# A graph network's attention layer: neighbour sums of all heads moved across the first head's steps

## The chip, the cores and the metric

One core of one Trainium2 chip. The metric is the device time of one execution of the whole kernel in microseconds (us): 1761.85 us, the median of three runs (1759.87 to 1763.0).

## The reference, cut to what matters

Four layers over a graph of 2708 nodes with 512 features: a normalisation with ReLU, then a graph layer whose result is added to `x`. Layers 0, 1 and 3 multiply the adjacency with features. Layer 2 is attention with 8 heads of 64 features:

```python
Wh = jnp.einsum('nd,hdo->hno', x, W)
f1 = jnp.einsum('hno,ho->hn', Wh, a1)
f2 = jnp.einsum('hno,ho->hn', Wh, a2)
e = jax.nn.leaky_relu(f1[:, :, None] + f2[:, None, :], negative_slope=0.2)
e = jnp.where(adj[None, :, :] > 0, e, -9e15)
attention = jax.nn.softmax(e, axis=-1)
h_prime = jnp.einsum('hnm,hmo->hno', attention, Wh)
```

The exponential of a leaky sum splits into products of exponentials of `f1` and of `f2`, joined by a maximum. So the kernel needs no exponential per pair of nodes: it makes a tile of weights by a maximum and a multiplication with the adjacency, and takes the softmax's denominator as a sum over the same tiles.

## The kernel before, in words

All four layers run on the one core, and the adjacency is kept on the chip as bytes (`vT`, turned, six groups). Nodes are cut into `NC = 22` chunks of 128, the last of 20.

**The dense stage of attention** (`stages2`, from `aggregate` and `staged`) goes over the chunks. `product2` multiplies by `W`, ScalarE evicts the product (`wh`, L1085), VectorE and POOL each multiply it with one of the vectors `a1`, `a2` (L1090), POOL folds its half (L1096), and `sums2` reduces (L1107) and clamps (L1109) into `f12`. `rows2` then takes exponentials for the first `EARLY = 11` chunks, turns them into a row on TensorE (`row2`, L1120: transpose into PSUM, copy L1122 on ScalarE, transfer L1123 to `rT` in memory), and loads that row spread over all partitions as `rb` (L957). At `LATE = 17` and after, it starts the first head: `scale` and `make` of its first steps run while the dense stage ends.

**The heads** are walked in `steps`: pairs of a unit `u` (a head, or one half of the columns of the first and of the last head) and a chunk `m`. The first head has two units of 22 steps, s0 to s21 with 1408 columns and s22 to s43 with 1300. Unit 2 is the first with the full width of 2708 columns. For each step:

- `scale` (L1028, L1030; ScalarE) scales the chunk's features and a constant block by `ef`: tile `whs`, four buffers;
- `make` (L1043; VectorE) writes the weights `t2 = max(rb, ec) * vT`: `TILES = 4` buffers;
- `compare` (L1061; ScalarE) makes a mask of comparisons, in middle heads only, for the chunks in `BY_SIDE`, 17 of the 22;
- `multiply` (L1243; TensorE) adds the products to `av` and `sums` in PSUM;
- `multiply_sides`, in the middle heads, gets the rest of the sums from the masks of the step before.

**The neighbour sums** serve the middle heads. Each chunk in `BY_SIDE` needs its `vT` in 16-bit form: four casts for four column ranges (`mask`, L1330, tiles of tag `x` with `XBUFS = 5` buffers), then eight matmuls (`count_neighbors`, L1342) against `parts2`, into two PSUM banks `adj_sums` that stay open from the first chunk to the last. `split` (L1292 to L1313) prepares `parts2`: it cuts `ef` and `ec*ef` each into three 16-bit parts (`parts`), with casts on ScalarE and subtractions on VectorE, then rearranges them.

**The tails**: the last chunk, of 20 rows, of the six middle heads is handled as one tile of 120 rows. `load_tails` loads it by many small transfers on SP's queue, `exp_tails` (L987 to L989) takes exponentials and scales, `make_tails` (L992) makes its weights. Step s44 is the first to use them.

**What sets the order.** The Python loop over steps issues `scale(s+3)`, `make(s+3)`, `compare(s+1)`, `multiply(s)`, and then what the table `plan` has under `s` (`behind(s, fn, ...)`). A scheduler then orders each engine's instructions by their issue order and readiness; each engine runs its list in that order. `tc.issue_after(ins)` keeps the instructions in its block behind `ins` on the same engine. PSUM has eight banks (pool `ps`): a half unit holds three, a full unit five, the neighbour sums two, and each row transpose one.

Of the kernel before, what the change touches and what calls it, by code (L numbers as in the profile page):

```python
# [8 lines left out]
F32 = mybir.dt.float32  # L9
F32R = mybir.dt.float32r  # L10
BF16 = mybir.dt.bfloat16
# [3 lines left out]
AF = mybir.ActivationFunctionType  # L15
ALU = mybir.AluOpType
# [4 lines left out]
P = 128  # L21

R = 128
# [21 lines left out]
def fast_layers(  # L45
# [36 lines left out]
    nc = tc.nc  # L82
    N, D = x_in.shape
    H, _, O = w2.shape
    NC = -(-N // R)
# [26 lines left out]
    EARLY = NC // 2  # L112
# [10 lines left out]
    common = ctx.enter_context(tc.tile_pool(name="common", bufs=2))  # L123
# [279 lines left out]
    vT = []  # L403
# [69 lines left out]
    with ExitStack() as ring_ctx:  # L473
# [31 lines left out]
        with tc.tile_pool(name="l0", bufs=2) as wk, ExitStack() as ctx_l0:  # L505
            units = [(g, m) for g in range(len(groups)) for m in range(NC)]
            tiles, acc, sums, xs = {}, {}, {}, {}
# [210 lines left out]
            first = [first_dense(lag, fn) for lag, fn in dense(x_in, product0, rows_of=paired)]  # L718
# [182 lines left out]
    BY_SIDE = [m for m in range(NC - 1) if m % 5 != 2]  # L901


    STEEP = 2.0**62
    ABOVE = 1.0 + 2.0**-21
# [32 lines left out]
    ef = at.tile([R, NC, H], F32, name="ef")  # L938
    ec = at.tile([R, NC, H], F32, name="ec")
    eb = at.tile([R, NC, H], F32, name="eb")  # L940
    parts = at.tile([R, NC * H * 8 + S], BF16, name="parts")
    nc.gpsimd.memset(parts, 0.0)
    parts_of = parts[:, : NC * H * 8].rearrange("p (m h k) -> p m h k", h=H, k=8)

    parts2 = at.tile([R, len(BY_SIDE), 2, H, 3], BF16, name="parts2")
    nc.gpsimd.memset(parts2, 0.0)
    one6 = at.tile([R, S], F32, name="one6")
    nc.gpsimd.memset(one6, 0.0)
    nc.gpsimd.memset(one6[:, 6:7], 1.0)
    row, weight, wh, whs, acc, sides, made = {}, {}, {}, {}, {}, {}, []  # L950

    def load_row1(h, lo, hi):

# [65 lines left out]
    def scale(s):  # L1019

        u, m = steps[s]
        h, q = units[u][0], rows(m)
        if in_tails(u, m):
            whs[s] = tails_w[:LINES, middle.index(h)]
            return
        t = at.tile([R, O + S], F32, name="whs", bufs=4)
        by = ef[:q, m, h : h + 1]
        nc.scalar.activation(t[:q, :O], wh.pop((u, m))[:q], AF.Copy, scale=by)  # L1028
        if not by_side(u, m):
            nc.scalar.activation(t[:q, O:], one6[:q], AF.Copy, scale=by)  # L1030
        whs[s] = t[:q]

    def make(s):
        u, m = steps[s]
        h, lo, hi = units[u]
        q = rows(m)
        g, k = where[m]
        if in_tails(u, m):
            weight[s] = tails_row[:LINES]
            made.append(made[-1])  # L1040
            return
        t = at.tile([R, N], F32, name="t2", bufs=TILES)
        ins = nc.vector.scalar_tensor_tensor(  # L1043
            t[:q, : hi - lo],
            row[h][:q, lo:hi],
            ec[:q, m, h : h + 1],
            vT[g][:q, k, lo:hi],
            op0=ALU.max,
            op1=ALU.mult,
        )  # L1050
        weight[s] = t[:q]
        made.append(ins.ins)
# [77 lines left out]
        nc.scalar.activation(ec[:, cs], f12[:R, cs, H:], AF.Exp, scale=SLOPE2 - 1.0)  # L1130


    LATE = NC - 5
    early_rows = [(0, EARLY // 2 + 1), (EARLY // 2 + 1, EARLY)]

    def rows2(c):
        for first, end in early_rows:
            if c == end - 1:
                exps_nodes(slice(first, end))
            for n in range(2):  # L1140
                if first <= first + 2 * (c - end + 1) + n < end and c >= end - 1:
                    row2(first + 2 * (c - end + 1) + n)
        if c == EARLY + 1:
            load_row1(*units[0])

        if c == LATE:
            exps2(slice(0, EARLY))
            load_wh(0)
            load_wh(GROUP)
        if LATE < c <= LATE + 3:  # L1150
            scale(len(made))
            make(len(made))

    def save_last2(c):
        if c < len(spans[-1]):
# [131 lines left out]
                    t[j * step : j * step + height, : b - a],  # L1287
                )

    def split():  # L1290

        nc.scalar.mul(eb, ec, -STEEP * ABOVE)  # L1292
        rest = common.tile([P, D], F32, name="rest", tag="t", bufs=3)
        rest = rest[:R, : NC * H].rearrange("p (m h) -> p m h", h=H)
        for i in range(2):
            e = ef
            if i:
                nc.vector.tensor_tensor(rest, ec, ef, ALU.mult)
                e = rest
            for k in range(3):  # L1300
                part = parts_of[:, :, :, 3 * i + k]
                nc.scalar.copy(part, e)
                if k < 2:
                    nc.vector.tensor_tensor(rest, e, part, ALU.subtract)
                    e = rest
        for i, heads in enumerate((slice(1, H), slice(1, H - 1))):
            kinds = sorted({m % 5 for m in BY_SIDE})
            for r in kinds:
                ms = [m for m in BY_SIDE if m % 5 == r]
                src = parts_of[:, r : ms[-1] + 1 : 5, heads, 3:6]  # L1310
                at_i = [BY_SIDE.index(m) for m in ms]
                assert at_i == list(range(at_i[0], at_i[-1] + 1, len(kinds)))
                nc.scalar.copy(  # L1313
                    parts2[:, at_i[0] : at_i[-1] + 1 : len(kinds), i, heads], src
                )


    fourths = [0, cut // 2, cut, (cut + N) // 2, N]
    counted, masks = [], {}

# [3 lines left out]
    def mask(i, j):  # L1324
        m = BY_SIDE[i]
        q = rows(m)
        g, k = where[m]
        own = slice(fourths[j], fourths[j + 1])
        t = masks[i, j] = common.tile([P, D], F32, name="x", bufs=XBUFS).bitcast(BF16)
        nc.scalar.copy(t[:q, : own.stop - own.start], vT[g][:q, k, own])  # L1330

    def count_neighbors(i):
        m = BY_SIDE[i]
# [37 lines left out]
    def behind(s, fn, *args):  # L1371
        plan.setdefault(s, []).append((fn, args))
# [3 lines left out]
    for c in range(EARLY, NC):  # L1376
        behind(4 + (c - EARLY) // 2, row2, c)
    behind(10, load_row1, *units[1])
    behind(9, split)
    behind(12, load_tails)  # L1380
    behind(18, exp_tails)
    behind(22, make_tails)
    behind(30, load_l3_weights)
    behind(30, spread_nodes)
    for u in range(2, len(units)):
# [3 lines left out]
        behind((u + 1) * NC - 1, evict, u, 0)  # L1389
        behind(min((u + 1) * NC, len(steps) - 1), evict, u, 1)  # L1390
    for i in range(len(BY_SIDE)):
        first = 11 + 7 * i // 4
        for j in range(4):
            behind(first + j // 2, mask, i, j)
        behind(first + 2, count_neighbors, i)
# [17 lines left out]
    for s in range(len(steps)):  # L1413
        if s == (len(units) - 3) * NC + 1:
            tails_ctx.close()
            e3_ctx = ctx.enter_context(ExitStack())
            e3 = e3_ctx.enter_context(
                tc.tile_pool(name="e3", bufs=2, side="right", reuse_waits="tile")
            )
        if s + 6 < len(steps) and (s + 6) % NC % GROUP == 0:  # L1420
            load_wh(s + 6)
        if s + 3 < len(steps):
            scale(s + 3)
            make(s + 3)
        if s + 1 < len(steps):
            compare(s + 1)
        multiply(s)
        multiply_sides(s - 1)
        for fn, args in plan.pop(s, ()):
            if fn in (load_l3_weights, spread_nodes, split):  # L1430
                with tc.issue_after(made[s]):
                    fn(*args)
            else:
                fn(*args)
# [742 lines left out]
```

## Time and profile before

| | |
|---|---|
| time, median of three | 1761.85 us |
| profiled execution | 1762.76 us, its span 1761.0 us |
| mean granted TensorE clock | 0.994 |
| TensorE busy | 1729.5 us (98%) |
| VectorE busy | 1307.4 us (74%) |
| ScalarE busy | 849.1 us (48%) |
| POOL busy | 249.2 us (14%) |
| makes, L1043 | 214, together 510.7 us |
| casts for the neighbour sums, L1330 | 68, from 801.7 to 912.2 us |
| neighbour-sum matmuls, L1342 | 136, from 849.7 to 913.6 us |
| first matmul of s0 | 819.57 us |

In a view in order of time, a line has the start in us, the time from its start to its end, the engine, the source line, the operation, the tile written and those read, partitions and elements, and how many instructions were merged; in brackets stands how long the engine had been idle before and what ended that. In a list of waits, a line has the waiting engine and line, what it waited for, and the total in us, the times, and the longest. In a list of groups, the figures after the bar are busy time in us, mean ns of one, and the idle time before with what ended it. A busy TensorE isn't TensorE at its peak.

### The profile page before, as it was taken

To read this page: it belongs to the slowest core of one execution; us is meant where nothing else is said; L and a number is where in the kernel's file an instruction comes from. 1 tells how busy PE (TensorE), PEld (TensorE's weight loads), DVE (VectorE), ACT (ScalarE), POOL (GpSimd) and SP (SyncE) were. 2 spreads that over 40 slices of the span, in tenths; PEclk is the share of its full clock that TensorE was granted. 3 is DMA by queue.
4 is the path that set the end of the run, shared out by engine and by line. 5 is a ranking of instruction groups with operands and counts; after the bars stand their busy time and mean duration, and the time that the engine had idled before them with its cause. 6 is when DMAs were issued, how large, how long until landed. Compare 5 with 4: busy or idle time off the path is not lost.

```text
span 1761.0 us, 29469 instructions
## 1 busy us (share of the span) xinstructions
PE 1729.5 (98%) x11280; PEld 1055.1 (60%) x11280; DVE 1307.4 (74%) x1889; ACT 849.1 (48%) x1547; POOL 249.2 (14%) x252
## 2 busy tenths in 40 slices
PE   8999999999999999999999999999999999999998
PEld 5567777744458887644474554434434455588886
DVE  8649888955555556888799999999999777633334
ACT  5447666722210000265888888888794566400000
POOL 1003323311111112255000000000001222100000
PEclk9999999999999999999999999999999999999999
DMA  8436666455551111333420220122022444313221
GB/s 295 140 95 207 205 197 185 145 113 122 121 141 49 48 49 54 110 128 102 127 61 16 62 63 22 50 64 59 16 65 69 136 136 133 112 32 109 76 72 41
DMA packets 167227, 177.37 MB, mean 101 GB/s; under 512 B 84127, under 2 KB 106591, under 8 KB 166060
## 3 DMA queue, kind: packets, MB, share of 16 engines
q1 hardware_dynamic: 144428, 131.99, 26.5%
q10 hardware_dynamic: 18808, 33.37, 5.1%
q0 software_dynamic: 3840, 10.03, 1.4%
q8 instruction: 90, 1.47, 0.3%
q14 instruction: 61, 0.50, 0.1%
HBM read 111.64 MB, written 55.36 MB: 95 GB/s over the span
## 4 chain that ended last, share of the span: by engine, by line
PE 84%; DVE 10%; DMA 2%; ACT 2%; issue 1%; POOL 0%; SPq 0%; ACTq 0%; DVEq 0%; POOLq 0%
PE acc L424 32%; PE av L1243 19%; PE nb_ps L187 8%; PE sums L1243 5%; DVE t L1043 4%; PE h_ps L187 4%; PE self_ps L187 4%; PE line_ps L187 4%; PE wh_ps L187 3%; PE hT_ps L245 2%; DVE cum L555 2%; PE fused_ps L370 1%; DMA x<-x 1%; PE av_ps L1196 1%; PE adj_sums L1342 1%
## 5 line engine op out<-in xcount | busy, mean ns | idle before, releaser
L1043 DVE SCALAR_TENSOR_TENSOR t<-rb,ec,vT 128x2708 f32<-128x2708 f32 (+2 forms) x214 | 510.7, 2449 | 17.3 <-PE sums L1243 15.3
L1243 PE MATMUL av<-t,whs 128*32 128x451 f32 (+5 forms) x4432 | 430.2, 513 | 4.6 <-DVE f L1109 1.4
L424 PE MATMUL acc<-halves,kt 128*128 128x512 f32 x1848 | 426.3, 390 | 3.5 <-DVE kt L847 3.2
L424 PEld LDWEIGHTS acc<-halves,kt 128*128 128x128 f32 x1848 | 345.1, 188 | 81.4 <-DVE kt L847 8.6
L1061 ACT ACTIVATE b<-t,eb 128x2708 bf16<-128x2708 f32 (+1 forms) x119 | 285.1, 2396 | 36.6 <-DVE t L1043 36.5
L1243 PEld LDWEIGHTS av<-t,whs 128*32 128x32 f32 (+1 forms) x4432 | 171.1, 110 | 178.4 <-issue 140.4
L424 PE MATMUL acc<-halves,ar 128*128 128x512 f32 x924 | 246.2, 417 | 2.4 <-ACT ar L549 2.2
L424 PEld LDWEIGHTS acc<-halves,ar 128*128 128x128 f32 x924 | 173.3, 189 | 62.4 <-issue 22.2
L223 ACT ACTIVATE ln_rs<-ln_mv,eps 128x1 f32<-128x1 f32 x88 | 25.5, 294 | 319.2 <-DVE ln_mv L221 310.7
L847 DVE SCALAR_TENSOR_TENSOR kt<-lastr,index,vT 128x512 fp32r<-128x512 int16 (+3 forms) x154 | 112.4, 742 | 75.8 <-PE acc L424 75.4
L1494 DVE CAST kt<-vT 128x512 fp32r<-128x512 uint8 (+3 forms) x154 | 56.4, 368 | 131.4 <-PE acc L424 131.2
L1210 POOL TENSOR_SCALAR z<-y 128x512 f32<-128x512 f32 x22 | 44.1, 2003 | 644.6 <-DMA aT<-avT 520.3
L555 DVE TENSOR_TENSOR_SCAN cum<-ai,deg 128x512 int16<-128x512 int32 (+2 forms) x110 | 130.7, 1196 | 0.0
L598 ACT ACTIVATE cum<-cum,limit 128x512 int16<-128x512 int16 (+3 forms) x132 | 88.1, 668 | 50.1 <-DVE deg L563 48.0
L219 DVE BATCH_NORM_STATS2 ln_st<-x 128x6 f32<-128x512 f32 x88 | 60.3, 687 | 51.6 <-DMA x<-x 38.4
L1028 ACT ACTIVATE whs<-wh,ef 128x64 f32<-128x64 f32 x214 | 72.8, 344 | 52.6 <-PE sums L1243 18.7
L1243 PE MATMUL sums<-t,whs 128*32 128x325 f32 (+4 forms) x952 | 92.2, 448 | 0.0
L187 PE MATMUL nb_ps<-wfn,hT 128*128 128x512 f32 x168 | 78.1, 609 | 2.1 <-ACT hT L247 2.1
L187 PE MATMUL wh_ps<-w2s,hT 128*128 128x512 f32 x168 | 75.9, 594 | 0.2 <-ACT hT L247 0.2
L187 PE MATMUL h_ps<-w0s,hT 128*128 128x512 f32 x168 | 75.8, 594 | 0.0
L187 PE MATMUL nb_ps<-wn,hT 128*128 128x512 f32 x168 | 75.6, 592 | 0.0
L187 PE MATMUL self_ps<-wfs,hT 128*128 128x512 f32 x168 | 75.6, 592 | 0.0
(210 smaller groups left out, 1907.8 us busy)
## 6 DMA issues: line engine op xcount, KB each, us to landing
x<-x SPq DMA_DIRECT2D x105, 256.0 KB
ai<-in_adj SPq DMA_DIRECT2D x84, 256.0 KB
x<-x ACTq DMA_DIRECT2D x84, 256.0 KB
x<-in_x SPq DMA_DIRECT2D x42, 256.0 KB
rb<-rT SPq DMA_DIRECT2D x7, 1354.0 KB
wh<-whd SPq DMA_DIRECT2D x63, 96.0 KB
packed<-two POOLq DMA_DIRECT2D x44, 128.0 KB, 3.1
whd<-wh SPq DMA_DIRECT2D x21, 256.0 KB
```

Of the source, the lines that this page charges most:

```text
L187: nc.tensor.matmul(po[:n], lhsT[:, f, :n], w[:, f, :], start=(f == 0), stop=(f == NF - 1))
L219: nc.vector.bn_stats(st[:n], xc[:n])
L424: nc.tensor.matmul(acc[:R], weight[:, k * R : (k + 1) * R], parts[:, i, :], start=(m == 0 and i == 0), stop=(m == NC - 1),)
L555: nc.vector.tensor_tensor_scan(cum[:n, :gw], ai[:n, :gw], ai[:n, :gw], 0.0 if g == 0 else deg[:n, m : m + 1], op0=ALU.add, op1=ALU.max,)
L598: nc.scalar.activation(cum[:n, :gw], cum[:n, :gw], AF.Sign, bias=limit[:n], scale=-1.0, accum_out=signs[:n, m, g : g + 1],)
L847: nc.vector.scalar_tensor_tensor(by_chunk(kt, cs), lastr[:, cs[0] * R : (cs[-1] + 1) * R].rearrange("p (c r) -> p c r", r=R), index[:R, m ...
L1028: nc.scalar.activation(t[:q, :O], wh.pop((u, m))[:q], AF.Copy, scale=by)
L1043: ins = nc.vector.scalar_tensor_tensor(t[:q, : hi - lo], row[h][:q, lo:hi], ec[:q, m, h : h + 1], vT[g][:q, k, lo:hi], op0=ALU.max, op1=AL ...
L1061: nc.scalar.activation(b[:q, : hi - lo], weight[s][:, : hi - lo], AF.Sigmoid, bias=eb[:q, m, h : h + 1], scale=STEEP,)
L1210: nc.gpsimd.tensor_scalar(z, y, 0.0, None, op0=ALU.min)
L1243: nc.tensor.matmul(p[j * S : (j + 1) * S, : b - a], lhsT, rhs[:, part * size + a : part * size + b], start=(s % NC == 0), stop=(s % NC == ...
L1494: nc.vector.tensor_copy(by_chunk(kt, cs), pattern(m, cs))
```

## The change

- `split` takes a range of chunks and runs twice: for the first 11 from `rows2`, in the dense stage at chunk `LATE + 1 = 18`, and for the other 11 at its former place, step 9.
- The neighbour sums of chunk `i` of the 17 begin at step `1 + 39 i // 16` in place of `11 + 7 i // 4`: two casts in that step, two in the next, the matmuls in the step after. They then stretch from s1 to s42 where they stretched from s11 to s41.
- The fourth of each chunk's casts (650 columns) goes to VectorE, into a tile of its own (`mask`, two buffers).
- Casts are kept behind the scaling and the make of the step two later (`scaled`, `made`).
- `exp_tails` is due at step 30 in place of 18, `make_tails` at 36 in place of 22.

```diff
     def scale(s):
...
-        nc.scalar.activation(t[:q, :O], wh.pop((u, m))[:q], AF.Copy, scale=by)
+        ins = nc.scalar.activation(t[:q, :O], wh.pop((u, m))[:q], AF.Copy, scale=by)
         if not by_side(u, m):
-            nc.scalar.activation(t[:q, O:], one6[:q], AF.Copy, scale=by)
+            ins = nc.scalar.activation(t[:q, O:], one6[:q], AF.Copy, scale=by)
+        scaled[s] = ins.ins
...
+    def split(first, end):
+
+        cs = slice(first, end)
+        nc.scalar.mul(eb[:, cs], ec[:, cs], -STEEP * ABOVE)
+        rest = common.tile([P, D], F32, name="rest", tag="t", bufs=3)
+        rest = rest[:R, : (end - first) * H].rearrange("p (m h) -> p m h", h=H)
+        for i in range(2):
+            e = ef[:, cs]
+            if i:
+                nc.vector.tensor_tensor(rest, ec[:, cs], e, ALU.mult)
+                e = rest
+            for k in range(3):
+                part = parts_of[:, cs, :, 3 * i + k]
+                nc.scalar.copy(part, e)
+                if k < 2:
+                    nc.vector.tensor_tensor(rest, e, part, ALU.subtract)
+                    e = rest
+        for i, heads in enumerate((slice(1, H), slice(1, H - 1))):
+            kinds = sorted({m % 5 for m in BY_SIDE})
+            for r in kinds:
+                ms = [m for m in BY_SIDE if m % 5 == r and first <= m < end]
+                src = parts_of[:, ms[0] : ms[-1] + 1 : 5, heads, 3:6]
+                at_i = [BY_SIDE.index(m) for m in ms]
+                assert at_i == list(range(at_i[0], at_i[-1] + 1, len(kinds)))
+                nc.scalar.copy(
+                    parts2[:, at_i[0] : at_i[-1] + 1 : len(kinds), i, heads], src
+                )
...
         if LATE < c <= LATE + 3:
             scale(len(made))
             make(len(made))
+        if c == LATE + 1:
+            split(0, EARLY)
...
-    def split():
...
     def mask(i, j):
...
+        n = own.stop - own.start
+        if j == 3:
+            t = masks[i, j] = tails.tile([P, fourths[1]], BF16, name="mask", bufs=2)
+            nc.vector.tensor_copy(t[:q, :n], vT[g][:q, k, own])
+            return
         t = masks[i, j] = common.tile([P, D], F32, name="x", bufs=XBUFS).bitcast(BF16)
-        nc.scalar.copy(t[:q, : own.stop - own.start], vT[g][:q, k, own])
+        nc.scalar.copy(t[:q, :n], vT[g][:q, k, own])
...
-    behind(9, split)
+    behind(9, split, EARLY, NC)
     behind(12, load_tails)
-    behind(18, exp_tails)
-    behind(22, make_tails)
+    behind(30, exp_tails)
+    behind(36, make_tails)
...
     for i in range(len(BY_SIDE)):
-        first = 11 + 7 * i // 4
+        first = 1 + 39 * i // 16
         for j in range(4):
             behind(first + j // 2, mask, i, j)
         behind(first + 2, count_neighbors, i)
...
             if fn in (load_l3_weights, spread_nodes, split):
                 with tc.issue_after(made[s]):
                     fn(*args)
+            elif fn is mask:
+                with tc.issue_after(scaled[s + 2]), tc.issue_after(made[s + 2]):
+                    fn(*args)
             else:
                 fn(*args)
```

More of the change, by code (lines that the diff above doesn't have):

```diff
@@ L949, in fast_layers @@
     nc.gpsimd.memset(one6[:, 6:7], 1.0)
-    row, weight, wh, whs, acc, sides, made = {}, {}, {}, {}, {}, {}, []
+    row, weight, wh, whs, acc, sides, made, scaled = {}, {}, {}, {}, {}, {}, [], {}
     def load_row1(h, lo, hi):
@@ L1288, in evict @@
                 )
-    def split():
[L1292 to L1315, printed above, removed]
     fourths = [0, cut // 2, cut, (cut + N) // 2, N]
```

## The prediction

> **What bounds the kernel now.** I read the page first (section 5: which engines carry attention), then the busy times by stage, then order of time around the first head. Steps are numbered s0 to s43 (two units of 22, half a head each), "make" is the VectorE weight tile of a step (L1043), "count" the eight neighbour-sum matmuls of one chunk (L1342), "cast" the byte-to-bf16 copy that feeds it (L1330).
>
> VectorE in order of time; the middle stretch and the start of the steady one:
>
> ```profile
> 879.55 9.79 DVE L1043 SCALAR_TENSOR_TENSOR t<-rb,ec,vT 128x1300 f32<-128x1300 f32 x6 [6.19 <-PE sums L1243]
> ...
> 912.05 29.59 DVE L1043 SCALAR_TENSOR_TENSOR t<-rb,ec,vT 128x2708 f32<-128x2708 f32 x10 [0.36 <-PE sums L1243]
> ```
>
> From 912.05 us, the make of s45 (first full-width tile), VectorE does not stop: the busy view gives it 387.95 of the 388 us from 912 to 1300, and it goes on to 1345. So the middle heads are VectorE's, and what the first head costs is the time at which VectorE can start s45. Before that it is held by TensorE, which has to give back one of the four weight tiles. Why TensorE is late (waits from 815 to 940, then TensorE and ScalarE in order of time):
>
> ```profile
> DVE t L1043 <- PE sums L1243: 15.3, 14, 6.2
> PE adj_sums L1342 <- ACT x L1330: 3.5, 7, 1.1
> ```
>
> ```profile
> 852.24 0.31 PE L1342 MATMUL adj_sums<-x,parts 128*24 128x352 bf16 x1
> 853.67 0.31 PE L1342 MATMUL adj_sums<-x,parts 128*24 128x352 bf16 x1 [1.11 <-ACT x L1330]
> ...
> 868.70 0.73 PE L1342 MATMUL adj_sums<-x,parts 128*24 128x352 bf16 x8
> ...
> 872.04 5.81 PE L1342 MATMUL adj_sums<-x,parts 128*24 128x325 bf16 x18 [0.24 <-ACT x L1330]
> 877.53 1.41 PE L1243 MATMUL av<-t,whs 128*32 128x325 f32 x16
> ```
>
> ```profile
> 871.24 5.99 ACT L1330 CAST x<-vT 128x650 bf16<-128x650 uint8 x9
> ```
>
> The 18 matmuls "busy" for 5.81 us run beside nine casts back to back for 5.99 us: they are paced by the casts. Elsewhere eight of them cost 0.28 to 0.30 us. TensorE loses about 8 us here, ScalarE being full and behind.
>
> [...]for 704 and 650 elements, the rows say 771 and 730, spaced 0.67. [...]
>
> ```profile
> L1494 DVE CAST kt<-vT 128x512 fp32r<-128x512 uint8 x88 | 37.3, 425 | 98.3 <-PE acc L424 98.3
> L1494 DVE CAST kt<-vT 128x128 fp32r<-128x128 uint8 x22 | 4.8, 226 | 4.8 <-PE acc L424 4.8
> ```
>
> 199 ns for 384 elements is 0.52 ns each[...]. The 16-element clamp L1109 takes 0.20 us alone and 1.23 behind a make while POOL works (812.19)[...].
>
> **Ledger of before.** From TensorE's start of s4 (828.70) to the end of s43 (917.28) is 88.6 us. Work: 18 steps of unit 0 at 1.775 (856.87 to 860.70 holds two and a count of 0.28) = 31.95; 22 of unit 1 at 1.64 = 36.1; 17 counts at 0.29 = 4.9; eleven row transposes at 0.22 (2.22 us for a step with two) = 2.45. Sum 75.4, so 13.2 us are stalls: 1.1 before the first count (849.1 to 850.5), 2.6 around the second (852.2 to 855.1), 7.9 between s21 and s22 (868.6 to 877.5 less 3.75 counts), 0.9 at 902, rest small. Every one waits for casts or for parts on ScalarE.
>
> **The change, part by part**, by the built order of each engine's instructions.
>
> *Casts spread and a fourth moved.* ScalarE loses 17 casts x 0.67 = 11.4 us. From 852 on it has 30 scalings x 0.45, 24 casts x 0.67, 1.1 for tails, 1.2 for evictions: 32 to 40 us of 53, so its cover for the rest is 13 us. VectorE gains 17 casts of 650 elements: 226 + 522 x 0.52 = 498 ns, less 0.08 overlap (makes of 1.67 follow each other by 1.596) = 0.42. Its bounds: [...]0.76 at one (159 + 650 x 1.05, the makes' slope, - 80); I take 0.42, as the nearest row has byte input too. With them VectorE needs 1.596 + 0.17 per step in unit 0 against TensorE's 1.775 + 0.12, and 1.49 + 0.17 in unit 1 against 1.64 + 0.12: still below, by 0.1, so hidden behind TensorE, but barely. If that cover goes, each cast costs its 0.42.
>
> *First half of the parts in the dense stage.* Five operations of 88 columns on VectorE, between 806 and 826: rows of 343 and 488 at 176 columns less 88 x 1.04, about 0.31 each, 1.55 in all. In this stretch VectorE is the chain (it waits for nothing but 0.80), so they count in full. ScalarE gets two short ones ahead of the row copy that precedes the first transfer of rb, against one scaling pair moved back: nothing to 0.2. The waits matter more. ScalarE's cast of the fourth rest now stands in front of the eviction wh L1085 of chunk 20, and it needs VectorE's subtraction behind two reductions, about 822.9; in before that eviction came at 818.40. Queued behind it are the evictions and the POOL product of chunk 20 (821.48 before, about 823.95 now), then POOL's remaining 1.1 + 1.26 + 0.72, on which VectorE's last reduction and the make of s4 wait: 826.89 becomes about 829.35.
>
> *First count at s3.* On TensorE it stands between s3 and s4, and its fourth operand is a VectorE cast placed behind the make of s5: 829.35 + 1.6 + 0.1 + 1.6 + 0.42 = 833.0. So s4 starts at 833.3 where it started at 828.70: **4.6 us paid**. Everything on TensorE queues behind that count. If its operand came in time I would pay 2 less.
>
> *s4 to s14.* Laid along the queues: second-half parts (same lengths, 1.55 on VectorE), eleven row copies, counts 1 to 4. The two count banks are now taken while row transposes run, leaving three PSUM banks, so a transpose waits for the row copy three before it; those go at about 1.5 us each (831.48 to 847.70 before, eleven). The eighth copy lands near 846, the last transpose could go at 846 to 847: a tie. I charge **0.9**.
>
> *Unit boundary.* ScalarE has evictions of unit 0 (0.4 x 3, the first from 0.6 before the end of s21) ahead of the scaling of s22: **0.8** on TensorE.
>
> *Tails later.* The exponentials leave the spot where ScalarE waited 2.6 us for tails_f; the row transposes behind it gain. The 3.03 us make of the tail rows stays between the makes of s25 and s26 in the built order, so despite its later due step it has the same place. VectorE, at its buffer limit, absorbs it: make of s26 at end of s21 + 6.4, needed at + 8.0.
>
> *Start of the steady stretch.* The first sigmoid (2.55) is now ahead of the eight count evictions (3.62), whose banks s44's sums need: s45's make ends at T + 3, then 2.55 + 3.62 = T + 9.2, so s44 ends near T + 9.9 and s45's products at T + 12.1, when the make of s49 wants that buffer at T + 11.8. **0.5**.
>
> *DMAs.* Same transfers; the er copy moves ahead of the second rb load in SP's queue, but waits only for the last row transpose, which rb's own rT rows need anyway. rb has some 4 us of slack. Nothing.
>
> Sum: 13.2 recovered, less 4.6 + 0.9 + 0.8 + 0.5 = 6.8: **gain 6.4, say 6.5 us**. By the other engine: from 830.9 VectorE has 17 x 1.596 + 22 x 1.49 + 17 x 0.42 + 1.55 + 2.95 = 71.5, so no earlier than 902.4; TensorE gives s45's buffer at about 904.9. The VectorE bound lies 2.5 below, so a larger gain than 10 is excluded.
>
> The profiled execution took 1762.76 us (span 1761.0 plus 1.8 outside), 0.9 above the median of 1761.85; the difference is applied to the median: 1755.3.
>
> **Rivals.** (A) *VectorE becomes the bound of the whole head.* For: its margin is 0.1 us a step. If a cast costs 0.76, 0.34 x 17 = 5.8 more VectorE work puts its bound at 908.2, s45 there: gain 3.3 after the 0.5, 1758.5; with ScalarE's waits on top, 1760. Against: L1494's slope. (B) *Gain eaten early.* If the mid-stage stall is re-formed by ScalarE being late with casts behind in-order waits (each scaling waits for TensorE, each part for VectorE), half of the 7.9 stays and I get 2 to 3 us: 1759 to 1761. For: ScalarE's order interleaves casts with row copies that wait for transfers. Against: its 13 us of room. (C) *Slower: row copies through three banks.* Place: s4 to s9. Price: eleven copies, eight of them ahead of the last transpose; each us more per copy costs 8. At 2.3 us a copy the gain is gone, above 2.7 the kernel is over 0.2% slower, about 1766 at 2.75. For: with two row buffers each copy waits for the transfer two before it (0.4 to 0.63 us seen each time). Against: 1.5 was measured with a 2.6 us wait in it. (D) *The change does not do what it says*: true for the tail make's place, not for the rest.
>
> **How the numbers follow.** My case (gain 4 to 10): 0.66. A: 0.14, half of it past 0.2%. B: 0.12, of which little counts as faster. C: 0.08. What a measurement tells from no change is 0.2%, 3.5 us, thus below 1758.3. Faster 0.66 + 0.07 + 0.01 = 0.74, same 0.18, slower 0.08. Range 1751 (VectorE's bound, cheap casts) to 1762 (B with nothing left); C and the farthest tails stay out. My own case alone: 1751.5 to 1758.
>
> **What would show it.** Right: no run of casts for 6 us with slow counts near 870; VectorE unbroken from about 905; a gap ahead of the first count near 827 to 833; VectorE casts of 0.50 us. Wrong: casts of 0.8 us; s4 later than 834; row transposes each waiting for ScalarE; or VectorE idle on TensorE in unit 1 for more than a us in one piece.

## The result: 2.6 us gained where 6.5 were forecast

The changed kernel takes 1760.18 us (median of 22 runs, 1755.38 to 1763.55), the kernel before 1762.64 on the same chip (22 runs, 1759.22 to 1765.34). The ratio is 0.9985, 95% interval 0.9978 to 0.9991: some 2.6 us less, between 1.6 and 3.9. The sign of the forecast holds, its size does not.

One thing has to be taken off before two traces are laid side by side. In the profiled execution of the changed kernel everything is already 1.48 us later at the row transposes near 790 us (791.88 for 790.40), before the first instruction that the change moves. TensorE's first product of s0 starts anywhere from 818.7 to 822.7 us over the profiles of this study, so below times are counted from that product: 819.57 us before, 821.05 after.

TensorE in order of time, changed kernel (start, length, engine, line, operation, count; in brackets the idle time before and what ended it):

```profile
828.57 0.31 PE L1350 MATMUL adj_sums<-x,parts 128*24 128x352 bf16 x2
834.03 0.43 PE L1350 MATMUL adj_sums<-mask,parts 128*24 128x325 bf16 x1 [5.14 <-DVE mask L1335]
...
834.28 2.80 PE L1274 MATMUL av<-t,whs 128*32 128x352 f32 x16
836.63 1.63 PE L1274 MATMUL sums<-t,whs 128*32 128x352 f32 x8
...
838.71 1.84 PE L1274 MATMUL av<-t,whs 128*32 128x352 f32 x16
...
841.68 1.36 PE L1274 MATMUL av<-t,whs 128*32 128x352 f32 x16
```

The same two steps in the kernel before:

```profile
828.70 1.39 PE L1243 MATMUL av<-t,whs 128*32 128x352 f32 x16 [1.44 <-DVE f L1109]
...
830.92 1.39 PE L1243 MATMUL av<-t,whs 128*32 128x352 f32 x16
```

Two things to see. The first count has begun by 828.57, and TensorE then stands still for 5.14 us until its fourth operand, a VectorE cast, is there: s4 starts 13.23 us after s0 instead of 9.13. And then the sixteen products of s4 take 2.80 us where the same sixteen took 1.39 before, and s5 starts 4.43 us after s4, before 2.22. The busy view of the changed kernel (stretch, its length, busy TensorE with instructions, granted clock, DMA share, GB/s) says why:

```profile
core 0: us, PE busy (x), PEclk, DMA share, GB/s
820.00:830.00 10.00, 8.89 (x115) 1.00 0.29 83
830.00:840.00 10.00, 5.97 (x43) 0.66 0.28 84
840.00:850.00 10.00, 10.00 (x132) 1.00 0.19 41
```

After the gap TensorE is granted 0.66 of its clock over this stretch. The kernel before has 1.00 there, but a drop of its own 40 us later (here with all engines, each with its busy time and its instructions):

```profile
core 0: us, PE busy (x) PEld busy (x) DVE busy (x) ACT busy (x) POOL busy (x), PEclk, DMA share, GB/s
830.00:840.00 10.00, 10.00 (x122) 3.36 (x117) 10.00 (x9) 5.36 (x22) 0.00 (x0) 1.00 0.16 33
...
870.00:880.00 10.00, 9.16 (x58) 3.17 (x61) 3.81 (x3) 10.00 (x21) 0.00 (x0) 0.66 0.65 198
```

In slices of 1 us both kernels have 6.8 us at half the clock between 815 and 930. In the kernel before they lie in the stall between s21 and s22, where TensorE is fed cast by cast and keeps up with the casts all the same (18 products in 5.81 us beside nine casts in 5.99), and s22 is then hardly slowed (1.41 us for its sixteen products, 1.38 for the next). In the changed kernel they fall on s4 and s5.

The rest is close to what was forecast. VectorE in order of time, changed kernel:

```profile
833.50 0.48 DVE L1335 CAST mask<-vT 128x650 bf16<-128x650 uint8 x1
833.90 3.26 DVE L1044 SCALAR_TENSOR_TENSOR t<-rb,ec,vT 128x1408 f32<-128x1408 f32 x2
...
876.66 3.03 DVE L992 SCALAR_TENSOR_TENSOR tails_row<-tails_row,tails_f,tails_v 120x2708 f32<-120x2708 f32 x1
...
909.21 11.89 DVE L1044 SCALAR_TENSOR_TENSOR t<-rb,ec,vT 128x2708 f32<-128x2708 f32 x4
...
921.88 20.76 DVE L1044 SCALAR_TENSOR_TENSOR t<-rb,ec,vT 128x2708 f32<-128x2708 f32 x7 [0.79 <-PE av L1274]
```

The waits from 815 to 940 (engine, line, what it waited for: us in total, times, longest), changed kernel:

```profile
PE adj_sums L1350 <- DVE mask L1335: 5.1, 1, 5.1
...
DVE t L1044 <- PE sums L1274: 3.6, 7, 0.9
...
PE adj_sums L1350 <- ACT x L1338: 0.6, 1, 0.6
```

VectorE's waits for TensorE fall from 15.3 us to 3.6, and TensorE's for ScalarE's casts from 3.5 to 0.6; the new one is the 5.1 us for the VectorE cast. The stall of 6.19 us near 879 is gone, and no run of casts holds TensorE there any more. s45's make comes at 909.21, which is 88.16 us after s0 (92.48 before): 4.3 us won. The next line is the stall at the start of the steady stretch, 0.79 us. At the end of the heads (the first division by the row sums) the lead is 3.4 us: 522.59 us after s0, before 526.02. What follows, up to the end, took 416.36 us here and 415.41 before; over the other profiles it lies between 413.6 and 416.9 with no relation to what was changed, so I put nothing on it.

### The profile page after: what moved, and what is told of

Read it like the earlier page. It is cut to its first block, busy times and chain, and to the rows that moved or that the text cites. A ratio compares the mean times of both kernels' runs of the same rounds, so it can differ in the third digit from the quotient of the medians.

```text
span 1760.0 us, 29461 instructions
## 1 busy us (share of the span) xinstructions
PE 1725.9 (98%) x11280; PEld 1072.8 (61%) x11280; DVE 1313.6 (75%) x1911; ACT 841.2 (48%) x1545; POOL 249.0 (14%) x252
## 3 DMA queue, kind: packets, MB, share of 16 engines
q8 instruction: 90, 1.47, 0.3%
## 4 chain that ended last, share of the span: by engine, by line
PE 82%; DVE 10%; issue 4%; DMA 2%; ACT 2%; POOL 1%; SPq 0%; ACTq 0%; DVEq 0%; POOLq 0%
PE acc L424 32%; PE av L1274 18%; PE nb_ps L187 7%; DVE t L1044 5%; PE sums L1274 5%; PE h_ps L187 4%; PE self_ps L187 4%; PE line_ps L187 3%; PE wh_ps L187 3%; PE hT_ps L245 2%; DVE cum L555 2%; PE fused_ps L370 1%; DMA x<-x 1%; PE av_ps L1227 1%; ACT b L1062 0%
## 5 line engine op out<-in xcount | busy, mean ns | idle before, releaser
L1274 PE MATMUL av<-t,whs 128*32 128x451 f32 (+5 forms) x4432 | 442.8, 514 | 3.5 <-DVE t L1044 1.2
L1274 PEld LDWEIGHTS av<-t,whs 128*32 128x32 f32 (+1 forms) x4432 | 189.8, 110 | 166.2 <-issue 113.2
L1274 PE MATMUL sums<-t,whs 128*32 128x325 f32 (+4 forms) x952 | 99.9, 449 | 0.0
L1274 PE MATMUL sums<-b,parts 128*32 128x338 bf16 (+2 forms) x884 | 76.7, 308 | 0.0
```

Source lines behind the costliest of these rows:

```text
L1274: nc.tensor.matmul(p[j * S : (j + 1) * S, : b - a], lhsT, rhs[:, part * size + a : part * size + b], start=(s % NC == 0), stop=(s % NC == ...
```

## The experiments

Every run is compared with the kernel before on its own chip. The last three columns come from the trace, in us from TensorE's first product of s0: the start of s4, that of the tails' first product (the end of the first head for TensorE), and the granted clock from 830 to 840. The last three kernels have 5 or 6 runs each, the others 9 to 22.

| kernel | ratio to before, 95% interval | s4 | tails | clock |
|---|---|---|---|---|
| before | 1 | 9.13 | 97.71 | 1.00 |
| changed | 0.9985 [0.9978, 0.9991] | 13.23 | 93.39 | 0.66 |
| e1_fill | 1.0006 [0.9999, 1.0014] | 13.31 | 99.46 | 1.00 |
| e7_fill_tails_late | 0.9985 [0.9976, 0.9993] | 13.17 | 93.60 | 1.00 |
| e8_tails_late | 0.9996 [0.9988, 1.0004] | 13.28 | 96.03 | 0.66 |
| e2_first_on_act | 0.9974 [0.9966, 0.9981] | 10.87 | 92.53 | 0.83 |
| e4_no_fourth | 0.9972 [0.9962, 0.9982] | 10.90 | 92.08 | 1.00 |
| e3_only_fourth | 0.9983 [0.9976, 0.9990] | 8.75 | 94.71 | 1.00 |
| e5_start3 | 0.9979 [0.9970, 0.9987] | 10.95 | 91.68 | 0.87 |
| e11_start3_tails_late | 0.9979 [0.9971, 0.9987] | 10.90 | 93.64 | 0.83 |
| e6_parts_later | 0.9974 [0.9964, 0.9984] | 11.08 | 92.72 | 0.83 |
| e14_parts_later_none | 0.9983 [0.9977, 0.9990] | 12.23 | 94.55 | 0.69 |
| e16_none_end3 | 0.9979 [0.9970, 0.9988] | 10.75 | 93.87 | 1.00 |
| e18_split4 | 0.9951 [0.9938, 0.9965] | 8.73 | 91.14 | 1.00 |
| e19_split4_none | 0.9963 [0.9951, 0.9976] | 9.50 | 91.50 | 1.00 |
| e20_split4_s10 | 0.9947 [0.9933, 0.9960] | 8.59 | 89.27 | 1.00 |

0.001 is 1.76 us. In e5_start3 and e14_parts_later_none a part of the slow stretch lies ahead of 830 us (0.96 and 0.97 from 820 to 830), so that their 0.87 and 0.69 stand for as long a stretch as 0.83 and 0.66 elsewhere.

### Does the slow clock cost what is missing? Fill the gap

Twenty matrix products of the identity with itself, which nothing reads, keep TensorE at work until the first count can run.

```diff
+    FILL = 20
...
+            warm = ps.tile([P, P], F32, name="warm", tag="ps")
+            for k in range(FILL):
+                nc.tensor.matmul(warm, ident, ident, start=(k == 0), stop=(k == FILL - 1))
```

> The changed kernel with twenty spare 128x128 matmuls (identity by identity, into a PSUM tile that nothing reads) on TensorE between s3 and the first count, where it stood idle for 5.14 us; about 4.3 us of work, so it should end before the VectorE cast arrives, and no wait is moved. Theory 1 (the gap lets TensorE's clock drop, and s4 and s5 then run slow: 4.43 and 2.67 us against 2.22 each in before): the sixteen products of s4 take 1.4 us instead of 2.80, s5 starts 2.2 to 2.7 us earlier relative to s0, the kernel takes about 1757.7, 2.0 to 2.7 us less than the changed one (ratio to before about 0.9972). Theory 2 (VectorE's makes, casts and tail in the second unit set the end of the first head): s45's make no earlier, 1760.2, ratio 0.9985. If the spare matmuls run late, slower.

TensorE of this run in order of time:

```profile
828.56 4.73 PE L1350 MATMUL warm<-ident 128*128 128x128 f32 x40
...
834.25 1.47 PE L1274 MATMUL av<-t,whs 128*32 128x352 f32 x16
...
839.08 1.36 PE L1274 MATMUL av<-t,whs 128*32 128x352 f32 x16
...
847.33 0.27 PE L1121 MATMUL f_ps<-ident,er 128*8 128x128 f32 x1 [2.06 <-ACT row L1123]
```

The clock stays at 1.00 from 820 to 860, s4 takes 1.47 us for 2.80, and s6 starts 4.83 us after s4 instead of 7.40: the clock is worth 2.6 us at this place. But the kernel becomes 3.7 us slower than the changed one, because the row transposes now wait for the row copies (4.5 us of TensorE's time, in four waits). ScalarE of this run in order of time, ACTq being its DMA issues:

```profile
836.84 0.41 ACT L1123 COPY row<-f_ps 8x128 f32<-8x128 f32 x2
839.88 1.28 ACTq L1124 DMA_DIRECT2D rT<-row  x2
841.22 0.32 ACT L1030 ACTIVATE whs<-one,ef 128x32 f32<-128x32 f32 x1 [3.96 <-DMA rT<-row]
...
844.69 0.26 ACT L1123 COPY row<-f_ps 8x128 f32<-8x128 f32 x1 [1.93 <-DMA tails_w<-one]
```

The copies are done at 837.2; their transfers are issued at 839.88, 2.6 us later, and ScalarE stands still for 3.96 us in all. In the changed kernel the same two copies come at 838.66 and are issued at 838.95. The order of ScalarE's instructions is the same in both. SP is issuing the loads of the tail rows at this time, and by the profile a later row copy is held for 1.93 us by one of these loads (`tails_w`). Why a row transfer on ScalarE's queue should wait for a load on SP's, the trace does not say. So the run mixes two effects, and its time says nothing on the first.

### The same with the loads of the tail rows out of the way

Filled as before, now into the count's own PSUM tile; the tail rows' loads are queued behind a later load of node features (made_wh holds those loads), and their scaling and make are kept behind those of steps 26 and 29. Counted from s0 the loads of the control then begin 16 us later than in the changed kernel, the scaling comes 21 us later and the make 9 us, between the makes of s29 and s30 in place of s25 and s26. e8_tails_late is the control without the filling products.

```diff
+        for k in range(FILL if i == 0 else 0):
+            nc.tensor.matmul(
+                counted[0][:, :P], ident, ident, start=(k == 0), stop=(k == FILL - 1)
+            )
...
+            elif fn is load_tails:
+                with tc.issue_after(made_wh[-1]):
+                    fn(*args)
```

> The changed kernel with the 20 filling matrix products ahead of the first neighbour count (into the count's own PSUM tile, which the count then starts afresh), and the loads of the tail rows queued behind a later load of the node features[...]; the scalings and the make of the tails come some ten steps later. Theory (slow TensorE clock after the 5.1 us gap costs 2.7 us, and the first fill run lost 6 us only because the row copies' transfers waited behind the loads of the tail rows): the clock stays at 1.00 between 830 and 840, no row transpose waits over 0.7 us for a row copy, the make of s45 comes some 85.5 us after the start of s0 (88.2 in the changed kernel), about 1757.5 us or 0.997 of the kernel before. Rival 1 (the row copies wait for the PSUM banks as such, whatever is loaded): 1763 to 1764 again, transposes waiting up to 2 us. Rival 2 (the second unit is paced by VectorE, so that nothing won at s4 reaches s45): make of s45 at 88 us, 1760 us.

> The changed kernel with the loads, scalings and make of the tail rows later in the same way, and no filling products: the control of the filled run. Theory (the tail rows are no part of what sets the end in the changed kernel, since its row copies arrive late enough to find their transfers free): within 0.7 us of the changed kernel, some 1760 us, 0.9985, the first count still 5.1 us late and the clock at 0.66 after it. Rival (the tail rows' make of 3.0 us and their 30 loads delay the second unit): 1757 us, 0.997.

Busy views, first the filled kernel, then the control:

```profile
830.00:840.00 10.00, 9.59 (x117) 1.00 0.41 122
```

```profile
830.00:840.00 10.00, 6.99 (x65) 0.66 0.44 143
```

TensorE in order of time, s4 and s6 of the filled kernel, then the control:

```profile
832.36 1.47 PE L1277 MATMUL av<-t,whs 128*32 128x352 f32 x16
...
837.19 1.36 PE L1277 MATMUL av<-t,whs 128*32 128x352 f32 x16
```

```profile
833.01 0.43 PE L1353 MATMUL adj_sums<-mask,parts 128*24 128x325 bf16 x1 [5.19 <-DVE mask L1338]
...
833.26 2.80 PE L1277 MATMUL av<-t,whs 128*32 128x352 f32 x16
...
872.72 3.00 PE L1277 MATMUL av<-t,whs 20*32 20x352 f32 x32 [0.82 <-ACT whs L1031]
```

s4 starts at nearly the same time in both (13.17 and 13.28 us after s0); after that the clock is 1.00 in one and 0.66 in the other. s6 starts 4.83 us after s4 with the filling and 6.77 without, so the clock is worth 1.9 us there. In the filled one no row transpose waits for a row copy. The tails' first product comes 2.43 us earlier (93.60 for 96.03), most of the rest being a longer wait for a cast in the control (0.66 us at 855.69, where the filled run has 0.16); s45's make and the end of the heads come 2.4 us earlier too. By the ratios the pair is 1.9 us apart, by the medians 1.3, with intervals that just overlap. Over the 13 runs of each the granted clock is 0.9957 in the mean with the filling and 0.9945 without, so the profiled executions are no exception.

Taken alone, the filled run looks like its second rival, by which VectorE paces the second unit: s45's make comes at 88.4 us and the ratio is 0.9985. The control rules that out, since without the filling s45's make comes 2.4 us later still: what is won at s4 does reach s45. This is the test that e1_fill was meant to be: the slow clock costs 1.9 us by s6 and 2.4 at the tails. It was made with the late tails; for the changed kernel itself e1_fill gives the price, 2.6 us by s6, but not how much of it reaches the end.

I had the control itself wrong. The later tails cost 2.6 us at the tails' first product, by a late scaling of s21 (0.82 us above), a second slow stretch after it (a clock of 0.83 from 870 to 880, in the filled run too) and a count waiting 1.02 us for a VectorE cast that stands behind the tails' make. Their place is not free. In the change, where only the due steps of scaling and make moved, no engine is seen waiting for the tails.

### Each part alone

```diff
-        if j == 3:
+        if j == 3 and i > 0:
```

> The changed kernel with the fourth cast of the first chunk alone back on ScalarE, so the first count no longer stands behind the make of s5 on VectorE. Theory 1 (the wait of the first count and the slow clock after it are what ate the gain): s4 starts about 2.4 us earlier relative to s0, at 10.8 us after it, the idle stretch falls from 5.14 to about 3 us, the clock holds or drops less; 1755.5 to 1758, ratio 0.996 to 0.9975. Theory 2 (VectorE bound in the second unit): within 1 us of the changed kernel, ratio 0.998 to 0.9985.

```diff
-        if j == 3:
+        if j == 4:
```

> The changed kernel with all casts on ScalarE, the rest of the change kept. Theory 1: as with the first chunk's cast alone put back, minus what ScalarE loses by 17 x 0.67 = 11.4 us more work out of about 13 us of room: 1756 to 1760. Theory 2 (VectorE's 17 x 0.40 us are what costs): the best of these four, 1754 to 1757. If ScalarE is what was short all along: stalls of counts on casts come back, 1760 or more.

The second one puts all casts on ScalarE. TensorE in order of time:

```profile
830.24 0.74 PE L1350 MATMUL adj_sums<-x,parts 128*24 128x352 bf16 x7
833.61 1.39 PE L1274 MATMUL av<-t,whs 128*32 128x352 f32 x16 [2.63 <-DVE t L1044]
...
838.50 0.27 PE L1121 MATMUL f_ps<-ident,er 128*8 128x128 f32 x1 [0.48 <-ACT row L1123]
...
851.82 0.44 PE L1350 MATMUL adj_sums<-x,parts 128*24 128x325 bf16 x5 [1.01 <-ACT x L1338]
```

With its four operands from ScalarE the first count is done before s4, and s4 waits only for its own make: 2.3 us earlier than in the changed kernel, at full clock. At s6 that is 4.3 us won (16.29 us after s0 for 20.63); at the tails 1.3 are left. The lines show part of where it goes: with s4 earlier, TensorE waits 1.2 us more for ScalarE's casts (1.01 and 0.17 us beside the 0.62 that the changed kernel has too). Step by step the lead is 3.7 us at s10, 2.5 at s11 and 1.6 at s13, so most of it goes at the two counts ahead of s11 and s13. e2_first_on_act is the same case with the cast of one chunk only; its clock drops, at s4 and again at s22 (0.83 from 830 to 840 and from 870 to 880). By the ratios the one VectorE cast ahead of s4 costs some 1.9 us, all seventeen 2.3; both intervals just overlap that of the changed kernel.

The other part alone, put into the kernel before:

```diff
+        if j == 3:
+            t = masks[i, j] = tails.tile([P, fourths[1]], BF16, name="mask", bufs=2)
+            nc.vector.tensor_copy(t[:q, :n], vT[g][:q, k, own])
+            return
```

> The kernel before with one part of the change alone: the fourth cast of every chunk on VectorE, start and spacing of the counts as before. Theory (VectorE's casts relieve ScalarE by 11 x 0.7 us where it is late, between s21 and s22, but each stands in a queue behind a make): the stall of 7.9 us between s21 and s22 falls to some 5, the other stalls stay, 1760 us, 0.9985. Rival (the casts alone are the gain of the change): 1757 us, 0.997. Other rival (they wait behind makes that wait for TensorE and hold the counts): slower by 1 us or more, 1764.

```profile
868.04 7.40 ACT L1335 CAST x<-vT 128x650 bf16<-128x650 uint8 x11
```

The run of casts between s21 and s22 is still there on ScalarE, but with three casts to a count it feeds three to four counts where nine casts fed two. The tails come 3.0 us earlier, the time is 3.0 us less: more than I expected, and as much as the whole change. So the two parts take from the same stall: alone 3.0 (casts) and 5.6 us (spread counts and split parts) at the tails, together 4.3. What is missing lies in large part where they meet, at the first count with its gap and its slow clock: with that one cast back on ScalarE (e2_first_on_act) it is 5.2.

### Later start, closer counts

Chunk i from step 3 + 37i/16, without and with the later tails:

> The changed kernel with the neighbour sums from step 3 + 37 i / 16 in place of 1 + 39 i / 16: the first count follows s5 instead of s3. Theory 1: s4 waits for its own make only, about 10.8 us after s0; idle stretch about 3 us; 1755.5 to 1758, ratio 0.996 to 0.9975. Theory 2: within 1 us of the changed kernel.

> The changed kernel with the first count two steps later (chunk i from step 3 + 37i/16) and the tail rows' loads, scalings and make later. Theory (what is left after the later start is a gap of 3.3 us ahead of s4 with a slow clock worth 1.2 us, and single waits for casts, none of which the tail rows cause): as with the later start alone, 1758.5 us, 0.998, within 0.7 us. Rival (the tail rows hold the row copies there too): 1756.5 us, 0.9965, with fewer waits of row transposes.

The first leads the changed kernel by 1.7 us at the tails; s4 again starts 10.95 us after s0 with a gap of 3.26 us ahead of it and sixteen products in 2.58 us. Its ratio, 0.9979, is just outside what the first theory gave. With the later tails 2.0 us are lost again, and a second slow stretch appears from 870 to 880 (0.83), both as in e8_tails_late, though the time doesn't show it (the same ratio for both).

```diff
-        first = 1 + 39 * i // 16
+        first = 1 + 36 * i // 16
```

> The changed kernel with all casts on ScalarE and the counts somewhat closer together (chunk i from 1 + 36i/16), so that the last count is over three steps before the tails and its evictions are done before the first sigmoid. Theory (the stall of 0.7 to 0.8 us at s45 is the tails' products waiting for the evictions of the counts): that stall goes, and the time is 0.5 to 0.8 us under the run with all casts on ScalarE, whose ratio was 0.9972; 0.9968, 1757.6 us. Rival (the stall comes from the sigmoid itself, ahead of whatever evictions there are): as that run, 0.9972, stall 0.7 us.

The stall at s45 did go: VectorE runs from s45 without a break. The time did not follow (0.9979 against 0.9972, intervals overlapping): this run has a stretch of slow clock at s22 (0.83 from 870 to 880, sixteen products in 2.13 us), and its tails are 1.8 us behind. The stall is explained, its worth is not shown.

### The parts out of the dense stage

```diff
-        if c == LATE + 1:
-            split(0, EARLY)
...
+    behind(2, split, 0, EARLY)
...
-        first = 1 + 39 * i // 16
+        first = 5 + 35 * i // 16
```

> The changed kernel with the first half of the parts split behind step 2, after the dense stage, and the counts from step 5 on (chunk i from 5 + 35i/16); a fourth of the casts on VectorE as in the change. Theory (the delay of s4 is the work of the parts in the dense stage, 1.9 us, and what the first count adds to it, 2.2 us, with a slow clock of 2.7 us after the gap): s4 starts some 9.3 us after s0 as in the kernel before (13.2 in the changed kernel), the clock stays above 0.9, the tails' first product comes some 91 us after s0 (93.4 in the changed kernel, 97.7 before), 1757 us, 0.9965. Rival (the parts and casts then fall together with the row copies on ScalarE, and the row transposes wait): s4 early, but 3 to 4 us of single waits between s4 and s14, 1760 us, 0.9985.

> The same with all casts on ScalarE. Theory (VectorE's casts cost more ahead of s4 than they save; with s4 early there is nothing left for them to delay): the two differ by under 1 us, 1757 to 1758 us, 0.9967. Rival (ScalarE, without VectorE's help, is late with casts in the first unit): 1.5 us or more slower than the kernel with a fourth on VectorE, 1759.5 us, 0.998.

Neither is a test of the parts: VectorE still does four of their five steps ahead of the dense stage's last clamp, and s4 starts 11.08 and 12.23 us after s0, behind gaps of 3.39 and 4.54 us ended by that clamp. The clock drops in both: 0.83 from 830 to 840 after the shorter gap, 0.97 and 0.69 from 820 to 840 after the longer, twice the loss. The two differ by 1.6 us by the ratios where under 1 was expected, but s4 alone is 1.15 us later in the second, so nothing follows on the casts. Behind step 4, with the counts from step 8, the order is free of them:

```diff
+    behind(4, split, 0, EARLY)
...
+        first = 8 + 32 * i // 16
```

> The changed kernel with the first half of the parts split behind step 4, so that none of its work on VectorE lies in the dense stage (in the earlier try the order of VectorE still held three of its steps there), and the counts from step 8 on (chunk i from 8 + 32i/16); a fourth of the casts on VectorE. Theory (s4 is late because the parts' work on VectorE and ScalarE is queued ahead of the dense stage's last sums): s4 starts 9.1 to 9.6 us after s0 as in the kernel before, with about 1 us of gap and the clock at 1.00; the tails' first product 90.5 us after s0 (93.4 in the changed kernel, 97.7 before); 1756 us, 0.9963. Rival (ScalarE is the limit from s4 on: parts, casts and row copies together hold the row transposes and the counts 3 us or more): s4 early, tails' first product at 92.5 to 93 us, 1758.5 us, 0.9978.

> The same with all casts on ScalarE. Theory of the ScalarE limit: without VectorE's fourth the casts are later, single waits of the counts in the second unit grow to 2 us or more in all, 0.0007 or more slower than its twin. Rival (the counts' spacing leaves ScalarE time enough): same within 0.0005, tails' first product 90.5 us after s0.

```diff
+        first = 9 + 30 * i // 16
```

> As the first of these with the counts from step 9 on and closer (chunk i from 9 + 30i/16), so that the last one is evicted before the tails. Theory: the stall of 0.8 us at s45 goes too; tails' first product 90.5 us after s0, 1755.5 us, 0.996. Rival (closer counts make TensorE wait for casts as in the kernel before): single waits of 1 us or more for casts between 870 and 905, 1758 us.

TensorE of e18_split4 in order of time:

```profile
828.25 1.39 PE L1272 MATMUL av<-t,whs 128*32 128x352 f32 x16 [1.04 <-DVE f L1110]
...
850.99 0.30 PE L1348 MATMUL adj_sums<-x,parts 128*24 128x325 bf16 x1 [2.23 <-ACT x L1336]
```

s4 is back where it was before the change, at full clock: the 4.1 us were the parts' work in the dense stage and the first count behind it (e5_start3, which moved the counts alone, took away 2.3 of them). One wait of 2.2 us for casts remains (ScalarE's part of the rival), and the clock drops after it: 0.83 from 850 to 860, and the next sixteen products take 2.33 us. The variant with all casts on ScalarE is 2.1 us behind by the ratios, within the intervals, so whether VectorE's fourth helps here stays open. e20_split4_s10 also loses the stall at s45 and has the full clock (1.00) from 820 to 920; its VectorE in order of time:

```profile
904.14 28.10 DVE L1044 SCALAR_TENSOR_TENSOR t<-rb,ec,vT 20x1300 f32<-20x1300 f32 x10
```

From s43's make on there is no break. It is the best kernel of the study: 0.9947 [0.9933, 0.9960], some 9 us less than before, against 2.6 for the change; its interval, from five runs, lies clear of the changed kernel's.

## Why the prediction was wrong, by its own steps

**What bounds, and the ledger.** Right in the sum, with one thing left unread, the clock (below). The 13.2 us of stalls were TensorE's waits for casts; in the changed kernel the waits for ScalarE's casts come to 0.6 us (one wait), and the lead at s45 goes through to the end of the heads but for the stall at s45.

**VectorE's casts.** Right: 0.48 to 0.50 us, a slot of 0.40 (833.50 to 833.90); forecast 0.50 and 0.42 from the slope of the final layer's casts (L1494); the makes' slope would have given 0.76, and the cheaper casts at the low end of the range were an estimate that no line shows. VectorE's pace stayed below TensorE's in the second unit, as the margin said: five makes and two casts take 8.2 us, and TensorE's five steps and two counts 8.8. Rival A, VectorE as the bound of the whole head, is out. But the margin was used up: the 3.03 us make of the tails sets VectorE back, from s25's make at 874.77 on it has no idle time up to the stall at 921, and it reaches s45's make at 909.21 just as TensorE is done with the tile (the last product of s40 ends at 909.17). Had TensorE won more after s25, s45's make could not have come earlier; that is read from the lines, no run tests it.

**First half of the parts, first count at s3.** The delay was right: the make of s4 1.9 us later (forecast 2.5), s4 4.1 us later (forecast 4.6), and e18_split4 shows that it comes from these two.

**The step that failed** is the same one's price, "4.6 us paid". It charged the gap by its length and everything after it at the usual rate. The change makes a gap of 5.14 us, and after it the trace has sixteen products in 2.80 us for 1.39 and a clock of 0.66; with the gap filled, the same products take 1.47 us at 1.00. I read that the gap would be there and didn't ask what TensorE would do after it, though the profile before shows such a drop (0.66 from 870 to 880) in the very stall that the ledger prices. The term put at nothing is 2.6 us by the lines of s4 and s5; the filled pair gives 1.9 by s6 and 2.4 at the tails. At the tails' first product the forecast lead was 13.2 - 4.6 - 0.9 - 0.8 = 6.9 us, the measured one 4.3: short by 2.6.

**s4 to s14, unit boundary.** Right in sum: s14 starts 22.3 us after s4 with the clock's part taken off; at the boundary TensorE waits 0.42 us for the scaling of s22 (forecast 0.8). Rival C (row copies hold the transposes) didn't happen in the change, but did in e1_fill, through the transfers behind the copies. C named these as what would slow the copies, but not the tail rows' loads that were under way.

**Tails later.** Right: the make stays between the same two makes (876.66) and waits for nothing; VectorE absorbs it, with nothing to spare (above).

**Start of the steady stretch.** Right in kind, 0.79 us for 0.5. e16_none_end3 and e20_split4_s10 show its cause, since it goes when the last count is evicted earlier.

**Rival B** (gain eaten by ScalarE being late) is not what happened in the change, though the measured time lies in its 1759 to 1761: the number fits it by chance. It may be the limit that stands next: e4_no_fourth gives back 3.0 of 4.3 us between s6 and the tails, 2.0 of it at the two counts ahead of s11 and s13.

## What to carry to other kernels

Price a new wait on TensorE twice: by its length, and by the slower products after it; here gaps of 5.1 to 5.2 us ahead of dense work cost 1.9 to 2.6 us more. Look for drops of the clock in the profile before, too. When two remedies take from the same stall, cost them together, and look at the one place where they meet: here one cast in VectorE's queue behind two makes cost some 1.9 us. Work put "early" is only free in a stage where its engines have slack; the same parts behind step 4, with the counts from step 8 or 9 on, gave the gain that the change was after (0.9951 and 0.9947 for 0.9985).

## What the runs showed of the hardware

- Here the clock drops in portions, and the gap doesn't decide alone. The views of 10 us show sixteen slow stretches in the sixteen profiles between 820 and 920 us. In slices of 1 us those of the kernel before and of the changed kernel go down to 0.50 and come to 6.8 us at half the clock. The other fourteen, if they too go down to a half, come by their views of 10 us to 3.4 us (twelve: 0.83, in e5_start3 0.96 and 0.87) or again to 6.8 (e8_tails_late 0.66, e14_parts_later_none 0.97 and 0.69). The four long ones lie after gaps of 5.14, 5.19 and 4.54 us ahead of s4, and in the stall of the kernel before. Gaps of 3.20 to 3.39 us and one of 2.23 us were followed by 3.4 us of it; gaps of 2.63 to 2.66 us once, and twice by none, with nearly the same instructions around them. So a gap of 2.23 us was enough in one run, and one of 2.66 was not in another.
- The slow stretch doesn't start at the same distance from the gap's start. In the changed kernel the half clock began 4.0 us after it; in e8_tails_late some 2.6, an estimate from the 1.94 us that s6 lost there (6.77 us after s4, for 4.83 with the filling) and 6.8 us at half the clock. So less of it fell on work there: in the changed kernel s6 came 7.40 us after s4. What sets the start, no run shows.
- It also dropped with hardly any gap: at s22, after 0.42 us of idle time, sixteen products took 2.09 us in e2_first_on_act and 2.13 in e16_none_end3 (a clock of 0.83 from 870 to 880 in both), and 1.30 in the changed kernel (1.00) after the same 0.42 us.
- The granted clock went with the spread of the times, too: of 52 runs of the kernel before on one chip, the 17 at 0.993 or 0.994 took 1764.2 us in the mean, and the 16 at 0.996 or 0.997 took 1761.6.
- In e1_fill transfers that one engine issues were held up while another engine's were under way: two row transfers on ScalarE's queue went out 2.6 us after their data was ready while SP was loading the tail rows, and ScalarE stood still for 3.96 us. In e7_fill_tails_late, with these loads later, no row transpose waits; it also leaves out the extra PSUM tile, so the loads alone are not shown to be the cause.
